# Moving the last five blocks of a routed expert layer into a conditional part

## The chip, the cores and the metric

The kernel runs on one core of a Trainium2 chip. The core has five engines that run their own instruction streams side by side: TensorE (PE in the profile, with its weight loads as PEld), VectorE (DVE), ScalarE (ACT), GpSimd (POOL) and SyncE (SP), which here issues most of the DMAs. The metric is the device time of one execution in microseconds. The kernel before took 1246.42 us, the median of three runs (1238.91, 1246.42 and 1249.45).

## The reference

The input x has 8 batches of 512 tokens with 512 features. Everything is fp32.

```python
xn = layernorm(x)
s  = gated_linear_attention(xn)     # 16 heads of 32, decay, chunks of 128, output projection
# the mixture, on the 4096 tokens of xn:
top4, e4 = top_k(softmax(xn @ gate_w.T), 4)          # 16 experts
w = top4 / top4.sum()
mixed  = sum over e of comb[:, e] * (silu(xn @ Wg[e]) * (xn @ Wu[e])) @ Wd[e]
shared = (silu(xn @ sWg) * (xn @ sWu)) @ sWd
ffn = mixed + shared * sigmoid(xn @ shared_gate_w)
out = x + s * silu(ffn)
```

Each token goes to 4 of 16 experts; an expert has two 512 to 128 matrices (gate and up) and one 128 to 512 matrix (down).

## The kernel before

The work stands in stages, written one after another in one function; a scheduling layer places the instructions of each engine and adds the semaphore waits.

The first stage normalizes all batches, writes the normalized rows to DRAM (`xn_d`), computes the router and the shared expert (kept in `sh_d`), and meanwhile runs attention for batch 0. `sort()` (L376 to 460) then works out where each of the 16384 (token, expert) pairs stands in lists that are sorted by expert. Each expert's list is padded to whole blocks of 128 rows, so the number of blocks that the lists fill depends on the data. The kernel provides for the most that can occur:

```python
NB = (B * N * TOPK + E * (P - 1)) // P      # L36: 143
```

In `sort()`, `nb` is the number of blocks of each expert and `end` (L412 to 414) their running sum, so that its last column is the number of blocks in use. From `end` it makes `eoff`, one expert number per block (held as the offset of that expert's weights, and as the column of its routing weight). `table()` makes `slot`, the token of each row of each block, while attention runs for batch 1.

The expert weights (`wexp`, 16 x 768 KB) are loaded in L969 to 970 and L979 to 980. Then comes the expert stage (L986 to 1100), one step for each of the 143 blocks, laid out as a software pipeline in the loop L1089 to 1098. For block i:

- `gather(i + 4)` (POOL): an indirect DMA fetches the rows of the block's 128 tokens. Seven buffers (`homes`) take turns.
- `turn_rows(i + 2)` (SP): a transposing DMA turns the 16-bit half of each row; `transpose_x(i + 2)` (TensorE) turns the fp32 half; `join(i + 1)` (ACT) puts both together as `xt`.
- `gate_up(i)`: TensorE loads the block's weight offset into a register (L1034) and multiplies (L1042, result `pgu`); ACT applies the Silu (L1046) and DVE the product (L1047), giving `slb`.
- `transpose_h(i - 1)`: TensorE turns `slb` (L1054), DVE copies it to `hT` (L1056).
- `down(i - 2)`: TensorE multiplies with the down matrix (L1063, `py`); DVE loads the column of the routing weight into a register (L1067) and scales the rows (L1072, `y`); SP stores them in `y_d` (L1074), 256 KB a block.

The `y` tiles come from the four buffers called `tmp`, which attention uses for its own scratch too.

The last stage (L1103 to 1207) runs attention for batches 2 to 7. It begins with `enter(2)`: keys (`pk`) and queries (`pq`) of batch 2 on TensorE (L598), with a Silu on ACT (L603) and a rotation on DVE (L605 to 609). Beside it `mixture` fetches the four expert rows of each token from `y_d` by indirect DMAs on POOL (L1121), adds them up, and `last` multiplies with the attention output and adds x. The transposed input of batch 3 (`xT_3`) is loaded by SP at the beginning of that stage (L538). All `y_d` gathers wait for the last stores to `y_d`. The order of each engine's instructions is that of the scheduling layer, except where a line says `behind(engine)` or `issue_after`, which pin an instruction behind an earlier one.

In the program as built, the first key matmuls of batch 2 stand before the last down projection of block 142 on TensorE, and the load of `xT_3` before the last store of `y` on SP.

Of the kernel before, what the change touches and what calls it, by code (L numbers as in the profile page):

```python
# [10 lines left out]
F32 = mybir.dt.float32  # L11
F16 = mybir.dt.float16
I32 = mybir.dt.int32
# [6 lines left out]
P = 128  # L20
B, N, D = 8, 512, 512
# [6 lines left out]
E, F, TOPK = 16, 128, 4  # L28
# [7 lines left out]
NB = (B * N * TOPK + E * (P - 1)) // P  # L36
WE = KC * 2 * F + D
TMP = 4
FIRST = 2
NBQ = -(-NB // 4)  # L40
QUAD = 4
GROUP = 16

# [51 lines left out]
def tile_block(ctx: ExitStack, tc: tile.TileContext, a: dict, out: bass.AP):  # L95
    nc = tc.nc
# [4 lines left out]
    const = ctx.enter_context(tc.tile_pool(name="const", bufs=1))  # L101
# [11 lines left out]
    y_d = dram.tile([NB * P, D], F32, name="y_d", tag="y_d")  # L113
# [23 lines left out]
    att = ctx.enter_context(tc.tile_pool(name="att", bufs=1, side="left"))  # L137
# [53 lines left out]
    sp = const.tile([P, 2, TOPK * NT], F16, tag="slot", name="sp")  # L191

    eoff = const.tile([P, 2, NBQ], I32, tag="eoff", name="eoff")

    def of_block(what, i):
        return eoff[i // NBQ * Q : i // NBQ * Q + 1, what, i % NBQ : i % NBQ + 1]
# [14 lines left out]
    def behind(engine):  # L211

        last = next(
            (i for i in reversed(nc.cur_bb.bb.instructions) if i.engine == engine), None)
        return tc.issue_after(last) if last else nullcontext()
# [160 lines left out]
    def sort():  # L376

        wt = p1.tile([P, NT, E], F32, tag="h1", name="wt", bufs=2)
        wr = p1.tile([P, NT, E], F32, tag="sl", name="wr", bufs=2)
        for r in range(TOPK):  # L380
            nc.gpsimd.tensor_tensor(
                wr if r else wt, oh[:, r].rearrange("p e t -> p t e"),
                w4[:, :, r : r + 1].to_broadcast([P, NT, E]), ALU.mult)
            if r:
                nc.gpsimd.tensor_tensor(wt, wt, wr, ALU.add)
        nc.sync.dma_start(
            xn_d[:, 2 * D :].rearrange("(t p) e -> p t e", p=P),
            wt.bitcast(U16))
        mf = mask.rearrange("p e t -> p (e t)")
        total = p1.tile([P, E * NT], F32, tag="lT", name="total", bufs=1)  # L390
        at = p1.tile([P, E, NT], F32, tag="at", name="at")
        af = at.rearrange("p e t -> p (e t)")
        for to, by, name in ((total, ones, "total"), (af, tri, "before")):
            ps = bank("a", f"p{name}")
            with on_pe():
                nc.tensor.matmul(ps, lhsT=by, rhs=mf, start=True, stop=True)
            nc.scalar.copy(to, ps)
        yield
        incl = p1.tile([P, E, NT], F32, tag="incl", name="incl")
        fl = incl.rearrange("p e t -> p (e t)")  # L400
        with behind(DVE):
            nc.vector.tensor_tensor_scan(fl, reset, total, 0.0, ALU.mult, ALU.add)

        ci = p1.tile([P, E], I32, tag="ci", name="ci")
        with behind(DVE):
            nc.vector.tensor_scalar(ci, incl[:, :, NT - 1], float(P - 1), None, ALU.add)
        with behind(DVE):
            nc.vector.tensor_scalar(ci, ci, 7, None, ALU.logical_shift_right)
        nb = p1.tile([P, E], F32, tag="nb", name="nb")
        with behind(DVE):  # L410
            nc.vector.tensor_copy(nb, ci)
        end = p1.tile([P, E], F32, tag="end", name="end")  # L412
        with behind(DVE):
            nc.vector.tensor_tensor_scan(end, ones[:, :E], nb, 0.0, ALU.mult, ALU.add)
        with behind(DVE):
            nc.vector.tensor_tensor(nb, end, nb, ALU.subtract)
        with behind(DVE):
            nc.vector.tensor_scalar(nb, nb, float(P), None, ALU.mult)
        yield

        with behind(DVE):
            nc.vector.tensor_tensor(fl, fl, total, ALU.subtract)
        with behind(DVE):
            nc.vector.tensor_tensor(af, af, fl, ALU.add)
        with behind(DVE):
            nc.vector.tensor_tensor(at, at, nb.unsqueeze(2).to_broadcast([P, E, NT]), ALU.add)
        yield
        oa = p1.tile([P, TOPK, E, NT], F32, tag="x", name="oa", bufs=3)
        pos = p1.tile([P, TOPK, NT], F32, tag="pos", name="pos")
        bl = p1.tile([P, 2, TOPK, NT], I32, tag="bl", name="bl")  # L430
        for r in range(TOPK):
            with behind(DVE):
                nc.vector.tensor_tensor(oa[:, r], oh[:, r], at, ALU.mult)
            with behind(DVE):
                nc.vector.tensor_reduce(
                    pos[:, r], oa[:, r].rearrange("p e t -> p t e"), axis=AX.X, op=ALU.add)
            with behind(DVE):
                nc.vector.tensor_copy(posi[:, r], pos[:, r])
            with behind(DVE):
                nc.vector.tensor_scalar(bl[:, 0, r], posi[:, r], P - 1, None, ALU.bitwise_and)  # L440
            with behind(DVE):
                nc.vector.tensor_scalar(bl[:, 1, r], posi[:, r], 7, None, ALU.logical_shift_right)
            with behind(DVE):
                nc.vector.tensor_copy(
                    sp.rearrange("p w (r t) -> p w r t", t=NT)[:, :, r], bl[:, :, r])
            yield

        cm = p1.tile([P, NBQ, E], F32, tag="xT1", name="cm", bufs=2)
        with behind(DVE):
            nc.vector.tensor_tensor(  # L450
                cm, end.unsqueeze(1).to_broadcast([P, NBQ, E]),
                iota_b.unsqueeze(2).to_broadcast([P, NBQ, E]), ALU.is_le)
        ef = p1.tile([P, NBQ], F32, tag="ef", name="ef")
        with behind(DVE):
            nc.vector.tensor_reduce(ef, cm, axis=AX.X, op=ALU.add)
        with behind(DVE):
            nc.vector.tensor_scalar(eoff[:, 0], ef, float(E - 1), float(WE), ALU.min, ALU.mult)
        with behind(DVE):
            nc.vector.tensor_scalar(eoff[:, 1], ef, float(E - 1), float(D), ALU.min, ALU.add)
        yield  # L460
# [507 lines left out]
    LATE = 4  # L968
    for e in range(E - LATE):  # L969
        nc.sync.dma_start(wexp[:, e, :], a["experts"][:, e, :])  # L970
    filling = table(wflat[:, (E - LATE) * WE :])
    next(filling)
    between[0] = lambda: next(filling, None)
# [5 lines left out]
    for e in range(E - LATE, E):  # L979
# [6 lines left out]
    blkp = left.enter_context(  # L986
        tc.tile_pool(name="blkp", bufs=1, side="left", reuse_waits="tile"))
    ROW = 2 * (D + E)
    more = att.tile([P, 2 * NC * D], U16, tag="v", name="more", bufs=2)
    homes = [blkp.tile([P, ROW], U16, tag=f"xg{j}", name=f"xg{j}") for j in range(4)]  # L990
    homes += [more[:, j * ROW : (j + 1) * ROW] for j in range(3)]
# [5 lines left out]
        return homes[i % len(homes)]  # L997

    def gather(i):
        if i < NB:  # L1000
            nc.gpsimd.indirect_dma_start(  # L1001
                out=row(i), out_offset=None, in_=xn_d,
                in_offset=bass.IndirectOffsetOnAxis(ap=slot[:, i : i + 1], axis=0))
# [2 lines left out]
        return pls[i % 2][:, i // 2 % 2]  # L1006

    def turn_rows(i):
        if i < NB:
            nc.sync.dma_start_transpose(turned(i), row(i)[:, D : 2 * D])  # L1010

    def transpose_x(i):
        if i < NB:
            pt_of[i] = bank("a", f"pt_{i}")
            for k in range(KP):
                nc.tensor.transpose(
                    pt_of[i][:, k * P : (k + 1) * P],
                    row(i).bitcast(F32)[:, k * P : (k + 1) * P], ident)

    def join(i):  # L1020
        if i < NB:
            xt = att.tile([P, KC, P], F32, tag="qT", name=f"xt_{i}", bufs=2)
            nc.scalar.copy(  # L1023
                xt[:, :KP, :].rearrange("p k t -> p (k t)"), pt_of.pop(i)[:, : KP * P])
            nc.scalar.copy(  # L1025
                xt[:, KP:, :].bitcast(U16).rearrange("p k (t h) -> p h k t", h=2),
                turned(i).rearrange("p (h k) t -> p h k t", h=2))
            xt_of[i] = xt

    def gate_up(i):  # L1030
        if not 0 <= i < NB:
            return
        with tc.issue_after(done[-1]) if done else nullcontext():
            _, (off_of[i],) = nc.values_load_multi_w_load_instructions(  # L1034
                of_block(0, i), engines=[mybir.EngineType.PE], min_val=0,
                max_val=(E - 1) * WE, bass_reorder=False,
# [11 lines left out]
        h_of[i] = sl  # L1048

    def transpose_h(i):  # L1050
        if not 0 <= i < NB:
            return
        ph = bank("a", f"ph_{i}")
        done.append(nc.tensor.transpose(ph[:, :P], h_of.pop(i), ident).ins)  # L1054
        hT = blkp.tile([F, P], F32, tag="hT", name=f"hT_{i}", bufs=2)
        nc.vector.tensor_copy(hT, ph[:, :P])  # L1056
        hT_of[i] = hT

    def down(i):
        if not 0 <= i < NB:  # L1060
            return
        py = bank("d", f"py_{i}")
        nc.tensor.matmul(  # L1063
# [22 lines left out]
            transpose_x(t - 2)  # L1086
    on_of.pop(FIRST - 1)
    join(0)
    for i in range(NB + 2):  # L1089
        turn_rows(i + 2)  # L1090
        join(i + 1)
        gate_up(i)
        if i == 2:
            gate_3(FIRST)
        transpose_x(i + 2)
        transpose_h(i - 1)
        down(i - 2)
        gather(i + 4)
    left.close()
    right.close()  # L1100

# [159 lines left out]
```

## Time and profile before

| | |
|---|---|
| median of three runs | 1246.42 us |
| profiled execution | 1229.7 us |
| its span, first to last instruction | 1227.9 us |
| mean granted TensorE clock | 0.991 |
| TensorE busy | 1177.3 us (96%) |
| VectorE busy | 768.2 us (63%) |
| GpSimd busy | 448.5 us (37%) |
| ScalarE busy | 407.3 us (33%) |
| expert matmuls L1042 | first 343.2 us, last 764.1 us |
| stores of y to `y_d`, issue to landing | 143, median 2.9 us |

In the profile a name such as `L1042 PE MATMUL pgu<-wexp,xt` is a group: line, engine, operation, written tile, read tiles. An entry of the order of time has the start, the length, the engine, the line and the count of merged records; a bracket says how long the engine stood idle before it and what released it. A fp32 matmul shows as two records, so that one block has eight `pgu` records and two `py` records. SPq, DVEq and the like are the instruction queue of an engine: register loads, semaphores and DMA issues, which are not counted as busy.

### The profile page before, as it was taken

To read this page: it belongs to the slowest core of one execution; us is meant where nothing else is said; L and a number is where in the kernel's file an instruction comes from. 1 tells how busy PE (TensorE), PEld (TensorE's weight loads), DVE (VectorE), ACT (ScalarE), POOL (GpSimd) and SP (SyncE) were. 2 spreads that over 40 slices of the span, in tenths; PEclk is the share of its full clock that TensorE was granted. 3 is DMA by queue.
4 is the path that set the end of the run, shared out by engine and by line. 5 is a ranking of instruction groups with operands and counts; after the bars stand their busy time and mean duration, and the time that the engine had idled before them with its cause. 6 is when DMAs were issued, how large, how long until landed. Compare 5 with 4: busy or idle time off the path is not lost. (4 is left out here: it accounts for less than half of the span.)

```text
span 1227.9 us, 21563 instructions
## 1 busy us (share of the span) xinstructions
PE 1177.3 (96%) x7799; PEld 696.7 (57%) x7799; DVE 768.2 (63%) x1652; ACT 407.3 (33%) x782; POOL 448.5 (37%) x430
## 2 busy tenths in 40 slices
PE   6998999989999999999999999999999999999997
PEld 3444554446467777777777776544554544445453
DVE  6378554899324444444444444887969789698784
ACT  3343333320264444444443443133141321411420
POOL 3222101100213333333333331581886857848211
PEclk9998999999999999999999999999999999999999
DMA  9784331181459999999999997950845636535012
GB/s 333 248 282 165 120 137 70 26 320 42 164 149 226 229 229 228 221 236 223 228 231 218 230 226 186 326 168 10 286 141 170 211 103 221 167 111 150 23 36 69
DMA packets 167719, 219.77 MB, mean 179 GB/s; under 512 B 93696, under 2 KB 102656, under 8 KB 165696
## 3 DMA queue, kind: packets, MB, share of 16 engines
q1 hardware_dynamic: 145936, 146.17, 40.3%
q0 software_dynamic: 21680, 72.23, 21.4%
q8 instruction: 64, 1.05, 0.3%
q14 instruction: 39, 0.32, 0.1%
HBM read 127.25 MB, written 72.35 MB: 163 GB/s over the span
## 5 line engine op out<-in xcount | busy, mean ns | idle before, releaser
L1042 PE MATMUL pgu<-wexp,xt 128*128 x1144 | 271.0, 380 | 2.4 <-ACT xt L1023 2.2
L1042 PEld LDWEIGHTS pgu<-wexp,xt 128*128 128x128 f32 x1144 | 216.5, 190 | 93.8 <-issue 31.4
L1001 POOL DMA_INDIRECT xg<-xn_d,slot x83 | 78.6, 947 | 281.0 <-DVE y L1072 168.1
L1047 DVE TENSOR_TENSOR slb<-slb,pgu 128x128 f32<-128x128 f32 x143 | 41.2, 288 | 205.8 <-ACT slb L1046 205.8
L1121 POOL DMA_INDIRECT yg<-y_d,posi x128 | 142.4, 1112 | 51.0 <-DMA m<-sh_d 23.5
L1025 ACT COPY xt<-pl 128x512 uint16<-128x512 uint16 x143 | 109.7, 767 | 148.5 <-DMA pl<-xg 92.1
L1063 PE MATMUL py<-wexp,hT 128*128 x286 | 146.4, 594 | 0.0
L556 PE MATMUL pv<-wv,xT 128*128 128x512 f32 x256 | 121.0, 611 | 4.3 <-DVE sh L370 2.6
L598 PE MATMUL pk<-xT,wk 128*128 128x512 f32 x256 | 121.9, 617 | 0.0
L598 PE MATMUL pq<-xT,wq 128*128 128x512 f32 x256 | 115.9, 593 | 0.0
L731 PE MATMUL pw<-wo,on 128*128 128x512 f32 x224 | 100.9, 596 | 1.8 <-ACT so L904 0.9
L1001 POOL DMA_INDIRECT more<-xn_d,slot x60 | 56.6, 943 | 115.9 <-DVE y L1072 111.2
L1153 POOL TENSOR_TENSOR xo<-xo,m 128x512 f32<-128x512 f32 x30 | 43.8, 1461 | 146.8 <-DVE m L1149 137.4
L1072 DVE TENSOR_SCALAR y<-py,xg 128x512 f32<-128x512 f32 x83 | 62.3, 750 | 30.4 <-PE py L1063 30.3
L556 PEld LDWEIGHTS pv<-wv,xT 128*128 128x128 f32 x256 | 46.4, 193 | 60.9 <-issue 55.2
L670 DVE TENSOR_TENSOR sc<-ps,dmask 128x512 f32<-128x512 f32 x128 | 79.4, 684 | 1.0 <-PE ps L654 1.0
L598 PEld LDWEIGHTS pq<-xT,wq 128*128 128x128 f32 x256 | 47.3, 191 | 52.2 <-issue 50.9
L598 PEld LDWEIGHTS pk<-xT,wk 128*128 128x128 f32 x256 | 46.9, 193 | 50.2 <-issue 47.7
L1046 ACT ACTIVATE slb<-pgu 128x128 f32<-128x128 f32 x143 | 39.8, 279 | 95.0 <-PE pgu L1042 94.9
L731 PEld LDWEIGHTS pw<-wo,on 128*128 128x128 f32 x224 | 41.2, 190 | 51.7 <-issue 44.7
L603 ACT ACTIVATE sk<-pk 128x512 f32<-128x512 f32 x32 | 19.1, 597 | 117.5 <-PE pk L598 102.1
L1072 DVE TENSOR_SCALAR y<-py,more 128x512 f32<-128x512 f32 x60 | 45.0, 750 | 19.8 <-PE py L1063 19.7
(166 smaller groups left out, 1751.1 us busy)
## 6 DMA issues: line engine op xcount, KB each, us to landing
y_d<-y SPq DMA_DIRECT2D x143, 256.0 KB, 2.9
wexp<-in_experts SPq DMA_DIRECT2D x16, 768.0 KB, 11.7
sh_d<-sh SPq DMA_DIRECT2D x32, 256.0 KB, 2.6
m<-sh_d SPq DMA_DIRECT2D x32, 256.0 KB, 4.5
xo<-in_x SPq DMA_DIRECT2D x32, 256.0 KB, 3.6
out<-xo SPq DMA_DIRECT2D x32, 256.0 KB, 2.1
x<-in_x SPq DMA_DIRECT2D x7, 1024.0 KB, 6.5
xT_d<-xT SPq DMA_DIRECT2D x7, 1024.0 KB, 5.1
```

The costliest lines, as they stand in the source:

```text
L556: nc.tensor.matmul(pv, lhsT=xT_of[b][:, k, t * P : (t + 1) * P], rhs=wv[:, k, :], start=(k == 0), stop=(k == KC - 1))
L598: nc.tensor.matmul(ps, lhsT=w[:, k, g * P : (g + 1) * P], rhs=xT_of[b][:, k, :], start=(k == 0), stop=(k == KC - 1))
L670: nc.vector.tensor_tensor(s, pss[j].rearrange("p (c t) -> p c t", t=C), dmask[:, g * HG + j].unsqueeze(1).to_broadcast([P, NC, C]), ALU.mult)
L731: nc.tensor.matmul(pw, lhsT=on_of[b][:, g, t * P : (t + 1) * P], rhs=wo[:, g, :], start=(g == 0), stop=(g == G - 1))
L1001: nc.gpsimd.indirect_dma_start(out=row(i), out_offset=None, in_=xn_d, in_offset=bass.IndirectOffsetOnAxis(ap=slot[:, i : i + 1], axis=0))
L1025: nc.scalar.copy(xt[:, KP:, :].bitcast(U16).rearrange("p k (t h) -> p h k t", h=2), turned(i).rearrange("p (h k) t -> p h k t", h=2))
L1042: nc.tensor.matmul(pg[:, : 2 * F], lhsT=xt[:, k, :], rhs=wflat[:, bass.ds(off + k * 2 * F, 2 * F)], start=(k == 0), stop=(k == KC - 1))
L1047: nc.vector.tensor_tensor(sl, sl, pg[:, F : 2 * F], ALU.mult)
L1063: nc.tensor.matmul(py, lhsT=hT_of.pop(i), rhs=wflat[:, bass.ds(off_of.pop(i) + KC * 2 * F, D)], start=True, stop=True)
L1072: gone.append(nc.vector.tensor_scalar(y, py, row(i).bitcast(F32)[:, bass.ds(at, 1)], None, ALU.mult).ins)
L1121: nc.gpsimd.indirect_dma_start(out=yg, out_offset=None, in_=y_d, in_offset=bass.IndirectOffsetOnAxis(ap=posi[:, r, g : g + 1], axis=0))
L1153: nc.gpsimd.tensor_tensor(xo, xo, m, ALU.add)
```

## The change

Blocks 0 to 137 are written out as before. Blocks 138 to 142 move into a part of the program that is entered only if the lists fill more than 138 blocks. For that, `sort()` keeps the number of blocks in use as an integer (`filled`), and after the first 138 blocks every engine loads it into a register and branches. Inside the part the pipeline is filled anew for the five blocks. Since the rows of those blocks in `y_d` would otherwise never be written when the part is skipped, they are filled with zeros earlier, after the first twelve expert loads, from a `tmp` tile that GpSimd clears.

In the program as built, every engine has the register load and the branch behind its work for block 137. On the path that skips the part each engine waits for its own last work, and SP for all of its DMAs, and then raises its semaphores to the values that the part would have left. The instructions of the last stage stand behind that on each engine; otherwise their order is that of before. The five stores of zeros stand on SP between the twelfth expert load and the load of `xT_2`.

```diff
+SURE = NB - 5
...
+    filled = const.tile([P, 1], I32, tag="filled", name="filled")
...
             nc.vector.tensor_tensor_scan(end, ones[:, :E], nb, 0.0, ALU.mult, ALU.add)
+        with behind(DVE):
+            nc.vector.tensor_copy(filled, end[:, E - 1 : E])
...
     for e in range(E - LATE):
         nc.sync.dma_start(wexp[:, e, :], a["experts"][:, e, :])
+    none = att.tile([P, D], F32, tag="tmp", name="none", bufs=TMP)
+    nc.gpsimd.memset(none, 0.0)
+    for i in range(SURE, NB):
+        nc.sync.dma_start(y_d[i * P : (i + 1) * P, :], none)
...
+    span = [0, SURE]
...
     def gather(i):
-        if i < NB:
+        if i < span[1]:
...
     def gate_up(i):
-        if not 0 <= i < NB:
+        if not span[0] <= i < span[1]:
             return
...
-    for i in range(NB + 2):
-        turn_rows(i + 2)
-        join(i + 1)
-        gate_up(i)
-        if i == 2:
-            gate_3(FIRST)
-        transpose_x(i + 2)
-        transpose_h(i - 1)
-        down(i - 2)
-        gather(i + 4)
+    def blocks(others=lambda i: None):
+        for i in range(span[0], span[1] + 2):
+            turn_rows(i + 2)
+            join(i + 1)
+            gate_up(i)
+            others(i)
+            transpose_x(i + 2)
+            transpose_h(i - 1)
+            down(i - 2)
+            gather(i + 4)
+
+    blocks(lambda i: gate_3(FIRST) if i == 2 else None)
+    _, (count,) = nc.values_load_multi_w_load_instructions(
+        filled[:1, :1], min_val=0, max_val=NB,
+        skip_runtime_bounds_check_because="the lists fill at most NB blocks")
+    with tc.If(count > SURE):
+        span[:] = SURE, NB
+        done.clear()
+        gone.clear()
+        for i in range(SURE, SURE + 4):
+            gather(i)
+        for i in range(SURE, SURE + 2):
+            turn_rows(i)
+            transpose_x(i)
+        join(SURE)
+        blocks()
```

The tests of the other helpers (`turn_rows`, `transpose_x`, `join`, `transpose_h`, `down`) change in the same way as those shown.

## The prediction

> **What bounds the kernel now.** I read the page's busy slices first, then a table of stretches, then the order of time around the end of the expert stage, then what TensorE waited for after it.
>
> From the page, the busy shares and the TensorE slices:
>
> ```profile
> PE 1177.3 (96%) x7799; PEld 696.7 (57%) x7799; DVE 768.2 (63%) x1652; ACT 407.3 (33%) x782; POOL 448.5 (37%) x430
> PE   6998999989999999999999999999999999999997
> L1042 PE MATMUL pgu<-wexp,xt 128*128 x1144 | 271.0, 380 | 2.4 <-ACT xt L1023 2.2
> ```
>
> TensorE is busy nearly everywhere, and the expert matmuls (L1042, eight records a block, 1144 / 8 = 143 blocks) waited 2.4 us in the whole stage. The stretches say the same of a middle piece of the stage and of its end (columns: busy us per engine with records, granted clock, DMA share, GB/s):
>
> ```profile
> 400.00:500.00 100.00, 99.99 (x445) 74.22 (x444) 41.73 (x104) 42.77 (x103) 32.07 (x34) 1.00 0.95 229
> 762.56:770.52 7.96, 7.96 (x26) 4.29 (x24) 3.69 (x7) 0.28 (x1) 0.00 (x0) 1.00 0.45 128
> ```
>
> The second row runs from the first matmul of block 142 to the first of the queries (pq) of batch 2: 7.96 us without a hole. The chain that ended last holds one DVE addition only, so I use the order of time instead:
>
> ```profile
> 691.24 1.89 PE L1042 MATMUL pgu<-wexp,xt 128*128 x8
> ...
> 743.71 1.89 PE L1042 MATMUL pgu<-wexp,xt 128*128 x8
> ...
> 749.54 1.89 PE L1042 MATMUL pgu<-wexp,xt 128*128 x8
> 752.67 1.99 PE L1042 MATMUL pgu<-wexp,xt 128*128 x8
> 756.84 1.99 PE L1042 MATMUL pgu<-wexp,xt 128*128 x8 [1.00 <-ACT xt L1023]
> 759.86 1.89 PE L1042 MATMUL pgu<-wexp,xt 128*128 x8
> 762.56 1.89 PE L1042 MATMUL pgu<-wexp,xt 128*128 x8
> ...
> 766.13 0.28 DVE L1056 COPY hT<-ph 128x128 f32<-128x128 f32 x1
> 766.23 1.02 PE L598 MATMUL pk<-xT,wk 128*128 128x512 f32 x2
> 767.09 1.02 PE L1063 MATMUL py<-wexp,hT 128*128 x2
> 767.94 2.74 PE L598 MATMUL pk<-xT,wk 128*128 128x512 f32 x6
> 768.15 0.75 DVE L1072 TENSOR_SCALAR y<-py,xg 128x512 f32<-128x512 f32 x1 [0.97 <-PE py L1063]
> ```
>
> From 691.24 to 749.54 lie 20 blocks: 58.30 / 20 = 2.915 us each. Late blocks 139 and 140 came 3.13 and 4.17 us after their forerunners, a hiccup of 1.5 us from late row transposes. Where the last block's down projection must wait for the DVE copy, TensorE runs the first two key matmuls of the next stage (pk at 766.23). After 765 us all idle time of TensorE matmuls sums to under 10 us, so time saved here should reach the end.
>
> **What the Trainium skill says.** "Advanced Engine Details and Errata", Control Flow Timing: a branch about 51 ns, a compare-and-branch about 108 ns; the trace of before shows neither. "DMA: Bandwidth & Descriptors", Latency and other measured facts: a register load has a floor near 600 ns; this trace differs (second row below, median 305 ns), and I use the trace. "Runtime: NRT & Kernel Launch", Instruction fetch mechanics: instructions stream in pages of 16 KB, 256 instructions, and a taken branch to a page that is not held waits for a DMA; the instruction queue of the trace fits the size (1.05 MB in 64 packets, 16.4 KB each), the stall no run here shows. "SBUF — State Buffer", Who interferes with whom: GpSimd and VectorE share one exclusive port pair, though a GpSimd instruction that only writes does not hold up the second operand of a VectorE one.
>
> ```profile
> L1072 DVEq EVENT_SEMAPHORE  x144: 21/50/50, 353.0 to 766.9; - x144
> L1067 DVEq TENSOR_LOAD <-eoff x143: 299/305/1021, 250.3 to 766.4; - x143
> ```
>
> **The change, part by part.** Is the part entered? Counting each token's four largest router logits on the reference's inputs, the experts get 929 to 1082 tokens; the counts rounded up to blocks of 128 sum to 136. 136 is not above 138: it is skipped.
>
> *Five blocks fewer.* 5 x 2.915 = 14.58 us of TensorE time off the path. Their gathers, row transposes and stores go too. Blocks 136 and 137 become the run-out, in the shape that 141 and 142 had.
>
> *The run-out loses its cover.* Let T0 be the first matmul of the last block. Before, T0 = 762.56; the last hT copy ends at 766.41 (T0+3.85), the last py then stands behind a key pair until T0+4.53, and pq starts at T0+7.96. In the changed program nothing from after the part may stand inside: order on TensorE is py_136, py_137, load of the count, branch, then pk. So py_137 starts about T0+4.0 and its record ends T0+5.05; its y multiply on DVE (0.75) ends T0+5.85. The skipping path adds waits: each engine waits for its own last work and then raises its semaphores to what the part would have left. The first pk waits for DVE's raised count, so for the last y. Behind DVE's wait no compute of DVE's is due, since its next work (swk) needs pk anyway. With 0.05 for each semaphore step (row above) pk starts at T0+6.1; eight passes at 0.43 (3.44 for the eight, from 767.94 + 6 x 0.43 = 770.52) bring pq to T0+9.55. Loss 9.55 - 7.96 = 1.6 us.
>
> *Load and branches.* DVE's load (0.305) and compare-and-branch (0.11) run on its sequencer while the 0.75 us multiply executes; TensorE's run beside it as well. Cost 0 with that cover, 0.4 us without. Bounds for fetching: below, nothing (a gain is excluded, nothing is removed); above, one landing of a store (2.9 us in the page's DMA list stands in for a page) for each of two taken branches on TensorE: pk at T0+10.4, so 4.3 more. The jump passes about 165 TensorE instructions (26 matmul and load records a block, plus registers), fewer than the 256 of a page, so I take zero, page presumably held.
>
> *SP and GpSimd at the part.* SP waits until the last y store has landed (issue about T0+6.0, plus 2.9), then releases GpSimd's gathers and the load of xT_3. Queued behind SP's wait: xT_3 and the m loads. xT_3 goes from T0+5.6 to about T0+9.3, 3.7 later, but its first reader (pv at 803.90) is 35 us off. The first yg gather was at 775.17 = T0+12.6 because the last store stood behind the 1 MB xT_3; now about T0+9.3, so GpSimd gets earlier, not later. ACT's first Silu needs HW semaphores SP raises about T0+8; pk's result comes at T0+9.6. Cost 0; if landings took 5 us more, ACT would be late by some 3.
>
> *Zero writes.* Five stores of 256 KB join SP's queue behind the first twelve expert loads (last issue about 263.5), ahead of xT_2 at 286.67. 1.31 MB at the 422 GB/s that the stretch 260 to 270 shows take 3.1 us in a queue idle for 23 us: cost 0, bounded by 3.1 if all of it delayed xT_2, for which TensorE already waits 1.66 us at 292.18. The GpSimd memset of the zeros (no row; a 128x512 addition there takes 1.46) runs beside DVE's mask work, which TensorE then waits for: 0 to 1.3, I take 0.1. The one-column copy on DVE: 0.18 as the neighbouring 128x16 subtraction, 0.1 of it exposed. Holding a tmp buffer delays nothing I find: its next user waits for the five stores about 35 us after they land.
>
> *Sum.* -14.6 + 1.6 + 0 + 0.2 = -12.8; I write -12.4, leaving 0.4 for the uncovered branch. The profiled execution takes 1229.7 us (span 1227.9, 1.8 around it), 1.3% below the median of the three runs, 1246.42, with no view telling why. Against itself it would fall to about 1217.3, or 1215.8 if its hiccup does not recur. Against the median: 1234.0.
>
> **Rivals.**
> *Page refetch* (25%): one or both taken branches wait for instructions. For: the jumps are the program's first inside it. Against: short jump. Gain 12.4 - 2.4 to 12.4 - 4.3: 1236 to 1239.
> *More than the sum* (14%): hiccups of 1.5 us and a slower steady pace in the timed runs go with the blocks, and earlier gathers help the last stage. For: blocks 139 and 140. Against: TensorE hardly waits later. Gain 14 to 16: 1230 to 1232.
> *Slower* (7%): after the branch each engine restarts its instruction stream cold. Place: between py_137 and pk. Price: serial fetches of 2.9 us on DVE, then TensorE, and again as they run on with no page ahead. From five such fetches in a row (14.5 us) it cancels the gain; eight give 1257. The part entered after all would end there too, through the same drain and a refill of gather (4.2), transpose (3.6) and joins: 1258. Against: 136 leaves two blocks of room.
>
> **How the numbers follow.** The forecast has 54%. A measurement of this kernel can tell about 1%, 12.5 us, from no change, and the forecast sits on that edge: half of its cases pass it, all of the second rival's do, the first's do not. Faster 0.45, same 0.48, slower 0.07. The three runs spread by 10.5 us, so I widen 1230 to 1239 by some 4 either way: 1226 to 1243.
>
> **What would show it.** Right: 138 blocks at 2.915; a hole in TensorE of about 0.3 us before py_137 and 1.2 us before pk; pk about 6.1 us after T0; first yg gather 9 to 10 us after T0. A hole of 3 us or more with no work beside it means fetching. Any pgu beyond 1104 records means the part was entered. A longer idle at 292 would blame the zero stores. Wrong altogether if idle time appears later, in TensorE's waits after the part, instead of the end moving in.

## The result and the profile after

Over six timed runs of each kernel, the kernel before took 1247.57 us (median, 1238.91 to 1251.24) and the changed one 1230.04 us (1228.61 to 1231.55): ratio 0.9869, 95% interval 0.9836 to 0.9902. That is 17.5 us less where 12.4 were forecast; the interval, 12.2 to 20.5 us, just takes the forecast in. The profiled execution of the changed kernel took 1229.93 us (span 1228.1), near its median, while that of the kernel before had taken 1229.7. So the two traces end at the same time although the timed runs differ by 17.5 us. Much of what follows is about that contradiction.

The page of the changed kernel, the busy shares, the TensorE slices and the group of the gate and up products:

```profile
PE 1170.0 (95%) x7734; PEld 690.8 (56%) x7734; DVE 754.3 (61%) x1638; ACT 401.5 (33%) x767; POOL 441.8 (36%) x426
...
PE   6998999989989999999999999999999999999997
...
L1051 PE MATMUL pgu<-wexp,xt 128*128 x1104 | 261.4, 380 | 0.8 <-ACT xt L1032 0.8
```

1104 / 8 = 138 blocks: the conditional part was skipped. The same line had 1144 records before. The next view has the two stretches that the prediction showed, a middle piece of the expert stage and the run-out from the first gate product of the last block (T0) to the first query product (pq) of batch 2:

```profile
400.00:500.00 100.00, 99.80 (x444) 74.28 (x443) 42.28 (x104) 42.92 (x102) 32.11 (x34) 1.00 0.94 229
746.29:756.50 10.21, 8.46 (x25) 4.12 (x24) 3.69 (x7) 0.28 (x1) 0.23 (x1) 1.00 0.29 105
```

The middle is as full as before. The run-out takes 10.21 us instead of 7.96, and TensorE is busy for 8.46 of them: a hole has come in. The order of time shows where:

```profile
746.29 1.89 PE L1051 MATMUL pgu<-wexp,xt 128*128 x8
...
749.09 2.22 PE L1072 MATMUL py<-wexp,hT 128*128 x4
...
751.36 0.75 DVE L1081 TENSOR_SCALAR y<-py,more 128x512 f32<-128x512 f32 x1 [0.45 <-PE py L1072]
...
752.99 3.67 PE L602 MATMUL pk<-xT,wk 128*128 128x512 f32 x8 [1.68 <-DVEq L1113]
...
756.27 0.95 POOL L1146 DMA_INDIRECT yg<-y_d,posi  x1 [19.25 <-SPq L1113]
756.50 1.02 PE L602 MATMUL pq<-xT,wq 128*128 128x512 f32 x2
```

The key products (pk) no longer stand between the last two down projections (py), and they start 6.70 us after T0 instead of 3.67. They were released by VectorE's queue at L1113, the line of the branch. The first gather of expert rows (yg) stands 9.98 us after T0, where the kernel before had it at 12.6. What VectorE's queue did in that time is in the view of the line of the load of the count (queue, operation, min/median/max in ns, first and last start in us), and in that of the branch:

```profile
L1110 POOLq TENSOR_LOAD <-filled x1: 497/497/497, 735.8 to 735.8; - x1
L1110 ACTq TENSOR_LOAD <-filled x1: 573/573/573, 748.2 to 748.2; - x1
L1110 PEldq TENSOR_LOAD <-filled x1: 486/486/486, 750.2 to 750.2; - x1
L1110 DVEq TENSOR_LOAD <-filled x1: 801/801/801, 751.4 to 751.4; - x1
L1110 SPq TENSOR_LOAD <-filled x1: 539/539/539, 752.5 to 752.5; - x1
```

```profile
L1113 PEldq COMPARE_BRANCH  x1: 368/368/368, 750.8 to 750.8; - x1
L1113 DVEq COMPARE_BRANCH  x1: 72/72/72, 752.6 to 752.6; - x1
```

VectorE's load starts with the last y product at 751.4 and takes 0.80 us, more than the 0.75 us that were to cover it. The branch follows at 752.6, the semaphore steps after it, and TensorE goes on at 752.99. Of the two holes that the prediction named, the one before the last py is 0.07 us (10.21 - 8.46 - 1.68; 0.3 forecast) and the one before pk 1.68 us (1.2 forecast). No engine shows a stall of microseconds that could be a fetch of instructions.

### The profile page after: what moved, and what is told of

The parts are those of the page before. It is cut to its first block, busy times and chain, and to the rows that moved or that the text cites. A ratio compares the mean times of both kernels' runs of the same rounds, so it can differ in the third digit from the quotient of the medians.

```text
span 1228.1 us, 21368 instructions
## 1 busy us (share of the span) xinstructions
PE 1170.0 (95%) x7734; PEld 690.8 (56%) x7734; DVE 754.3 (61%) x1638; ACT 401.5 (33%) x767; POOL 441.8 (36%) x426
## 5 line engine op out<-in xcount | busy, mean ns | idle before, releaser
L1051 PE MATMUL pgu<-wexp,xt 128*128 x1104 | 261.4, 380 | 0.8 <-ACT xt L1032 0.8
L1051 PEld LDWEIGHTS pgu<-wexp,xt 128*128 128x128 f32 x1104 | 209.0, 190 | 88.5 <-issue 42.8
L1010 POOL DMA_INDIRECT xg<-xn_d,slot x80 | 75.9, 949 | 248.5 <-DVE y L1081 162.5
L1034 ACT COPY xt<-pl 128x512 uint16<-128x512 uint16 x138 | 105.8, 766 | 140.2 <-DMA pl<-xg 86.8
L1072 PE MATMUL py<-wexp,hT 128*128 x276 | 141.3, 594 | 0.1
L560 PE MATMUL pv<-wv,xT 128*128 128x512 f32 x256 | 123.5, 622 | 5.2 <-DVE sh L372 4.1
L564 ACT COPY v<-pv 128x512 f32<-128x512 f32 x32 | 18.8, 588 | 122.2 <-PE pv L560 118.3
```

The source lines that it names most:

```text
L560: nc.tensor.matmul(pv, lhsT=xT_of[b][:, k, t * P : (t + 1) * P], rhs=wv[:, k, :], start=(k == 0), stop=(k == KC - 1))
L1010: nc.gpsimd.indirect_dma_start(out=row(i), out_offset=None, in_=xn_d, in_offset=bass.IndirectOffsetOnAxis(ap=slot[:, i : i + 1], axis=0))
L1034: nc.scalar.copy(xt[:, KP:, :].bitcast(U16).rearrange("p k (t h) -> p h k t", h=2), turned(i).rearrange("p (h k) t -> p h k t", h=2))
L1051: nc.tensor.matmul(pg[:, : 2 * F], lhsT=xt[:, k, :], rhs=wflat[:, bass.ds(off + k * 2 * F, 2 * F)], start=(k == 0), stop=(k == KC - 1))
L1072: nc.tensor.matmul(py, lhsT=hT_of.pop(i), rhs=wflat[:, bass.ds(off_of.pop(i) + KC * 2 * F, D)], start=True, stop=True)
```

## The experiments

Two theories stood after the result. *Sum*: the change is worth the time of five blocks less what the run-out grew, about 12.3 us, and the rest of the 17.5 is scatter. *More than the sum*: the kernel before loses time somewhere else too, and the change removes that. Three groups of four kernels were run, each group on one chip and beside the kernel before: on chips 11, 1 and 13, by the numbers of the record, where the kernel before takes 1229, 1247 and 1229 us. For the first comparison and for the profile of before no chip is noted. Each group ran at another time too, so whether such a level belongs to the chip is not shown; the text speaks of the lower and the higher level. In the tables, pk and pq are counted from T0, and "last stage" runs from that first pq to the end of the span, in the profiled execution.

**First group, where the kernel before takes 1229.28 us** (1225.44 to 1234.77, 19 runs).

| kernel | median us | ratio to before, 95% | pk | pq | last stage |
|---|---|---|---|---|---|
| before | 1228.69 | 0.9997, 0.998 to 1.0014 | 3.67 | 7.96 | 457.4 |
| changed | 1217.18 | 0.9898, 0.9873 to 0.9922 | 6.70 | 10.21 | 459.7 |
| changed, no branch | 1211.71 | 0.9863, 0.9832 to 0.9893 | 3.67 | 7.96 | 456.7 |
| changed, 136 blocks | 1210.23 | 0.9843, 0.9816 to 0.9869 | 6.70 | 11.90 | 461.2 |

*The kernel before against itself*, no edit.

> The kernel before, unchanged, against itself. Sum theory (the change is worth 14.6 us of blocks less the 2.25 us that the run-out grew, 12.3 us; the other 5 us of the 17.5 measured are scatter of the kernel before): ratio 1.000 with an interval of about 0.005 to each side, single times between 1229 and 1251 us, and the place of the scatter is the last stage (its length differs by up to 15 us between profiled executions, 457.4 us in the one shown, while the first 742 us differ by under 3). More-than-the-sum theory (the kernel before has a real loss that the change removes beside the blocks): its runs stay near 1246 us, the profiled execution shown (1229.7) was the outlier, and a new profile shows the loss.

The ratio is 1. But single times lie between 1225.06 and 1234.77, not up to 1251. Neither theory had that: the level of the kernel before had moved by 18 us. By its time (1229.7 us) and its last stage (457.4 us) the profile of before that the prediction used belongs to this level, not to that of the timed runs beside it.

*The changed kernel again*, no edit.

> The changed kernel, unchanged, once more. Sum theory: 12 to 13 us below the kernel before on the same chip (ratio 0.990), pq of the last stage 10.2 us after the first gate and up product of block 137's successor place, as in its first profile. More-than-the-sum theory: again 17 us below (ratio 0.986) and again a narrow spread of about 3 us against some 10 for the kernel before.

12.1 us below, and the run-out the same to 0.01 us: the sum's figure. The pair of traces accounts for it. T0 moved from 765.18 to 749.48 us (-15.70), the run-out grew by 2.25, the last stage by 2.3; together -11.2, the difference of the spans (1230.5 and 1219.3).

*Without load, test and conditional part*: the last five blocks are left out for good.

```diff
-    _, (count,) = nc.values_load_multi_w_load_instructions(
-        filled[:1, :1], min_val=0, max_val=NB,
...
-    with tc.If(count > SURE):
...
```

> The changed kernel without the load of the count, the test and the conditional part: 138 blocks always, the last five blocks are left out for good; the zero writes and the copy of the count stay. Theory that the load and the branch outlast the cover of the last y product: the first pk of the last stage comes 0.5 to 1.7 us sooner after the last block's first gate product than the 6.70 us of the changed kernel, the first pq as much (9.0 to 9.6 us instead of 10.21), and the time is 0.6 to 2 us below the changed kernel. Rival (the run-out without its cover costs this much by itself, the branch nothing): pk stays at 6.5 to 6.7 us and the time within 0.3 us.

The direction was right and the size was not: pq came 2.25 us sooner instead of 0.6 to 1.2, because with no branch the two key products go back between the last down projections. And the time fell by 5.5 us, not 2. So the branch costs more than its own hole. The two traces lie further apart than the medians, by 9.3 us, but 4.1 of that came ahead of T0, where the programs are alike (the changed kernel's trace has two more stretches of half clock there, each 3.4 us long, at 340 and 354 us). Behind T0 there is, beside the run-out, the last stage: 456.7 against 459.7 us. Its TensorE instructions are the same, in the same order, and the lag between the two traces grows at two places only before the 803 us mark of the changed kernel's trace: the transposes of the rotated keys (pk from kT) come 1.10 us late at 787 us and another 0.65 late at 800 us. The same waits recur in the third group, which is where I show them. Right behind them the clock record of this trace has half the clock for 3.4 us, at 801 us, which costs 1.7. With the 2.25 of the run-out and the 1.75 of the two waits that makes 5.7 us, near the 5.5 of the medians.

*136 blocks ahead of the test*, seven in the part.

```diff
-SURE = NB - 5
+SURE = NB - 7
```

> The changed kernel with 136 blocks ahead of the test instead of 138 (seven in the conditional part, still not entered, since 136 are filled). Sum theory: two blocks of 2.915 us less, 5.8 us below the changed kernel, and the run-out and the branch the same (pk at 6.7 us, pq at 10.2 us). More-than-the-sum theory, where what was gained beside the blocks came with the end of the stage moving away from a slow stretch of the last stage: the step is not 5.8 us but anything from 0 to 10, and the last stage's length changes with its start.

7.0 us below the changed kernel, 5.8 expected from two blocks. pk at 6.70 us is right; pq at 11.90 is off by 1.7, since a stretch of half clock (3.4 us from 747.6 us) fell on the eight key products, which took 5.37 us instead of 3.67.

**Second group, where the kernel before takes 1247.02 us** (1240.94 to 1257.27, 43 runs).

| kernel | median us | ratio to before, 95% | pk | pq | last stage |
|---|---|---|---|---|---|
| changed, gathers delayed | 1230.92 | 0.9861, 0.9834 to 0.9888 | 6.70 | 10.21 | 472.7 |
| changed, count loaded early | 1229.64 | 0.9866, 0.9836 to 0.9896 | 6.02 | 9.53 | 473.8 |
| 143 blocks, branch | 1246.15 | 0.9995, 0.9978 to 1.0013 | 3.67 | 7.96 | 472.1 |
| 143 blocks, zero writes | 1245.75 | 0.9984, 0.9963 to 1.0004 | 3.67 | 7.96 | 467.3 |

*Gathers delayed*, the question being whether the earlier gathers make the two waits.

```diff
             yg = comb.tile([P, D], F32, tag="yg", name=f"yg_{b}_{t}_{r}", bufs=14)
+            if (b, t, r) == (FIRST, 0, 1):
+                for _ in range(8):
+                    nc.gpsimd.memset(yg, 0.0)
```

> The changed kernel with eight memsets of 128x512 (0.52 us each by the one that the changed kernel has, 4.2 us in all) on GpSimd between the first and the second gather of expert rows in the last stage. Port theory (after the branch the gathers and with them GpSimd's sums of expert rows come about 4 us earlier against TensorE's work than in the kernel before; a sum that runs beside a two-input VectorE operation holds that one up for 2.1 us instead of 0.68, now on the way to TensorE): the sums stand again as in the kernel before, the two waits of TensorE for kT in the first batch of the last stage (1.0 and 0.65 us) are gone, and the time is 1.5 to 3.5 us below the changed kernel. Rival (the waits come from the branch itself or from the load of x that now comes 2 us later): they stay, and the time is that of the changed kernel or up to 1 us above it.

The gathers did move, the second from 1.0 us after pq, in the changed kernel's first trace, to 6.1, but the time is that of the changed kernel at this level (1230.04 us in the first comparison). It doesn't decide the matter. At this level the changed kernel has neither of the two waits in its first profile: other gaps (below) come before them, which would give VectorE the time. There was nothing here for the delay to remove. At the other level it wasn't tried.

*Count loaded early*, at block 100, on all five engines.

```diff
+        if i == 100:
+            with behind(DVE), behind(ACT), behind(POOL), \
+                    behind(mybir.EngineType.SP), behind(mybir.EngineType.PE):
+                counts.append(nc.values_load_multi_w_load_instructions(
+                    filled[:1, :1], min_val=0, max_val=NB, bass_reorder=False,
...
-    _, (count,) = nc.values_load_multi_w_load_instructions(
...
```

> The changed kernel with the count loaded into the registers of all five engines in the middle of the blocks (at block 100) instead of after the last one; the branch stays. Theory that the load of the count on VectorE (0.80 us in the trace) outlasts the last y product and so holds TensorE's first pk: pk at 6.1 us after the last block's first gate product instead of 6.70, pq at 9.6 instead of 10.2, and the time 0.6 us below the changed kernel. Rival (the branch itself is what holds it, or the time lies in the order of the instructions): pk stays at 6.6 to 6.7 us, the time within 0.3 us.

The run-out of this kernel in the order of time, and VectorE's branch:

```profile
744.52 1.89 PE L1051 MATMUL pgu<-wexp,xt 128*128 x8
...
749.58 0.75 DVE L1081 TENSOR_SCALAR y<-py,more 128x512 f32<-128x512 f32 x1 [0.45 <-PE py L1072]
...
750.54 3.67 PE L602 MATMUL pk<-xT,wk 128*128 128x512 f32 x8 [0.99 <-DVEq L1123]
...
754.05 3.17 PE L602 MATMUL pq<-xT,wq 128*128 128x512 f32 x7
```

```profile
L1123 DVEq COMPARE_BRANCH  x1: 72/72/72, 749.6 to 749.6; - x1
```

The branch now runs at 749.6, at the start of the last y product and beside it. pk is at 6.02 us and pq at 9.53, both 0.68 sooner, so the load was what outlasted its cover. The whole time can't show 0.7 us here.

*143 blocks and a branch*: the conditional part holds one memset and is not entered.

```diff
-    span = [0, SURE]
+    span = [0, NB]
...
     with tc.If(count > SURE):
-        span[:] = SURE, NB
...
-        blocks()
+        spare = blkp.tile([P, P], F32, tag="sl", name="spare", bufs=2)
+        nc.vector.memset(spare, 0.0)
```

> All 143 blocks as in the kernel before, then the load of the count, the test and a conditional part with one small memset, not entered; the zero writes stay (they are overwritten). Branch theory: pq of the last stage 10.2 us after the last block's first gate product instead of 7.96 (2.25 us), and the first batch of the last stage 1.6 to 3.3 us longer by earlier gathers: 4 to 5.5 us slower than the kernel before (ratio 1.003 to 1.0045). Sum theory of the prediction (the branch hides): within 1 us of the kernel before.

No cost of the branch can be seen (the interval is -2.7 to 1.6 us, where 4 to 5.5 were expected), and pq is at 7.96 us. The first gather of expert rows stands 4.5 us behind pq, as in the kernel before, so the second cost has no occasion here either. The reason is the place of the branch: this part uses nothing of the blocks, so the scheduler put the branch into the last blocks' work, with products queued behind it. The views of its two lines:

```profile
L1110 PEldq TENSOR_LOAD <-filled x1: 487/487/487, 765.0 to 765.0; - x1
L1110 DVEq TENSOR_LOAD <-filled x1: 537/537/537, 765.6 to 765.6; - x1
```

```profile
L1113 PEldq COMPARE_BRANCH  x1: 230/230/230, 765.6 to 765.6; - x1
L1113 DVEq COMPARE_BRANCH  x1: 72/72/72, 766.2 to 766.2; - x1
```

VectorE and TensorE load and branch here while TensorE's products follow one another without a hole: busy for all 7.96 us from T0 at 765.03. So it isn't the branch that costs 2.25 us in the changed kernel; it is that nothing from behind it can fill the run-out ahead of it, and that VectorE's load stands last.

*143 blocks with the zero writes*, the memset and the copied count, no branch.

> All 143 blocks, with the five zero writes, the memset and the copy of the count, without load, test and conditional part. Prediction's step (they hide): ratio 1.000, at most 0.3 us. Upper bound of that step: 3.1 us slower (ratio 1.0025).

Ratio 0.9984, at most 1.0004: the bound of 3.1 us (1.0025) is excluded, and the forecast of 0.2 us lies within the interval (-4.6 to 0.5 us). TensorE's wait for xT at 292 us was 1.0 us in this trace, 1.7 in that of before.

**Third group, where the kernel before takes 1228.68 us** (1225.27 to 1233.78, 19 runs).

| kernel | median us | ratio to before, 95% | pk | pq | last stage |
|---|---|---|---|---|---|
| before | 1229.90 | 1.001, 0.9995 to 1.0025 | 3.67 | 7.96 | 457.2 |
| changed | 1219.77 | 0.9925, 0.9902 to 0.9947 | 6.69 | 10.20 | 460.5 |
| changed, no branch | 1214.66 | 0.9876, 0.9848 to 0.9904 | 3.67 | 7.96 | 456.3 |
| 136 blocks, early count | 1213.65 | 0.9858, 0.983 to 0.9886 | 6.02 | 9.53 | 460.6 |

The kernel before, the changed one, the one without a branch, and 136 blocks with the early count (the two edits above together):

> The kernel before once more with a profile. The chips or placements behind the two calls so far differ: where the kernel before takes 1229 us its profiles show a last stage of 457.4 us, where it takes 1247 us the profiles of the other kernels show last stages of 467 to 474 us, with gaps of 0.3 to 0.7 us before TensorE's small matmuls in which it waits for nothing that the profile shows. Theory that this is a property of where the program runs, whatever the kernel: at 1247 us this profile too has the gaps and a last stage of 467 to 474 us; at 1229 us it has none, and 457 us. Rival (the gaps come with the zero writes, the branch or the gathers): 457 us in both places.

> The changed kernel once more beside it. Where the kernel before takes 1229 us: 12 us below it, last stage 459 to 461 us by waits of 1 to 1.7 us for VectorE's rows that run into GpSimd's sums. Where it takes 1247 us: 16 to 17 us below it, last stage 470 to 474 us; the profiles then tell how much of the difference lies ahead of the last stage (13 to 15 us by the counts so far) and how much in it.

> 138 blocks with no load of the count, test or conditional part (the last five blocks are left out), once more beside the changed kernel. Branch theory: 2.25 us sooner at the first pq of the last stage in either place, and the last stage shorter by the 1.6 us of waits for VectorE's rows where these can be seen: 3 to 6 us below the changed kernel. Rival (the 5.5 us of the first comparison was chance of the throttle): 2 us or less.

> 136 blocks ahead of the test, seven in the conditional part, and the count loaded in the middle of the blocks. Sum theory: 5.8 us for the two blocks and 0.7 us for the load, 6.5 us below the changed kernel, and 18 to 24 us below the kernel before, by the place. Rival (two blocks nearer to the end of the filled ones bring a new wait): less than 4 us below the changed kernel.

The level was again the lower one, so the kernel before gave no profile at 1247 us. At 1229 us its last stage takes 457.2 us without gaps, as expected. The changed kernel is 8.9 us below it, 12 expected (interval 6.5 to 12.0). Without the branch it is 5.1 us better, inside the expected 3 to 6, so the 5.5 of the first group recurs; of the two differences (5.2 and 5.0 us in the means) 1.7 and 1.9 us go with the granted clock, by the estimate below, and 3.5 and 3.1 us do not. 136 blocks with the early count are 6.1 us below the changed kernel, 6.5 expected.

What TensorE waited for in the first batch of the last stage, from its first pq to the next batch's, by the table of waits (us in total, times, longest). The kernel before:

```profile
PE pk L625 <- DVE state L659: 1.6, 1, 1.6
```

The changed kernel:

```profile
PE pk L629 <- DVE state L663: 3.3, 2, 2.3
```

The changed kernel without a branch:

```profile
PE pk L629 <- DVE state L663: 1.3, 1, 1.3
```

One wait of 1.3 to 1.6 us without the branch, two of together 3.3 us with it: 1.7 us more than in the kernel before, in this group as in the first. The new one is the first, 1.03 us; the other is 0.65 us longer than before. What releases them is VectorE's state update (L663), which reads the tile pk that the transposes are to overwrite. It stands behind VectorE's row of operations on keys and queries. Ahead of the place of the new wait the row reads in the kernel before (order of time, from 20 us after pq):

```profile
791.21 0.69 DVE L609 TENSOR_TENSOR kT<-kT,swk 128x512 f32<-128x512 f32 x1
...
794.25 2.15 DVE L609 TENSOR_TENSOR qT<-qT,swq 128x512 f32<-128x512 f32 x1
794.57 1.28 POOL L1127 TENSOR_TENSOR yg<-yg,yg 128x512 f32<-128x512 f32 x1
```

and in the changed kernel:

```profile
774.42 2.06 DVE L613 TENSOR_TENSOR kT<-kT,swk 128x512 f32<-128x512 f32 x1
774.63 1.29 POOL L1152 TENSOR_TENSOR yg<-yg,yg 128x512 f32<-128x512 f32 x1
...
778.59 1.28 POOL L1155 TENSOR_TENSOR yg<-yg,yg 128x512 f32<-128x512 f32 x1
778.87 1.56 DVE L613 TENSOR_TENSOR qT<-qT,swq 128x512 f32<-128x512 f32 x1
...
780.92 0.52 DVE L663 SCALAR_TENSOR_TENSOR state<-state,lamc,pk 128x32 f32<-128x32 f32 x2
...
781.50 0.33 PE L629 MATMUL pk<-ident,kT 128*128 128x128 f32 x1 [1.03 <-DVE state L663]
```

The same two-input operation takes 0.69 us alone and 2.06 us when a GpSimd sum of expert rows runs inside it. The Trainium skill, "SBUF — State Buffer", Who interferes with whom, has the two engines share one exclusive port pair, and the numbers agree with that: 0.69 + 1.29 = 1.98. (It is VectorE's operation that is held up, though by the trace it started 0.21 us before the sum.) In the kernel before one operation of this row was hit; with the branch GpSimd's work starts earlier against TensorE's (the first gather 0.10 instead of 4.62 us after pq, the first sum 9.46 instead of 12.44), and two are hit ahead of a transpose that TensorE is waiting for. That the earlier gathers are the cause is read from the traces, and without the branch both the early gathers (first at 4.5 us after pq again) and the new wait are gone. But that run takes the branch away with them, and the one that was to delay the gathers alone fell where the waits don't show, so it is not shown by an experiment of its own.

**What stays open.** At the higher level all five profiles I have (the changed kernel's first and the second group's four) have last stages of 467 to 474 us, and TensorE's waits over that stage show gaps ahead of small products. The changed kernel:

```profile
PE pk L647 <- issue: 5.0, 12, 0.5
PE ps L658 <- issue: 3.4, 11, 0.5
```

143 blocks with a branch:

```profile
PE po L692 <- issue: 2.6, 4, 1.0
PE ps L658 <- issue: 2.1, 6, 0.9
PE pk L647 <- issue: 1.9, 5, 0.5
```

"issue" means that TensorE waited for nothing that the profile shows. None of the nine profiles at the lower level has such gaps in the last stage, whatever the kernel. They go with the level of the run and not with the change, since the 143-block kernels have them too; what they are, the records don't say. A profile of the kernel before at this level is missing.

Why the gain is larger at this level the traces don't tell: between the two 143-block kernels of the second group (spans 1245.1 and 1236.7) and the changed kernel's first profile (1228.1) they give 17.0 and 8.6 us, while the medians give 16.1 and 15.7. The timed runs tell more, since each has its mean granted clock on record. Span times (1 - clock) is an estimate of what stretches of half clock took from a run. Averaged over the runs it is:

| | before, mean us | clock's share | changed, mean us | clock's share | gain | gain without the clock's share |
|---|---|---|---|---|---|---|
| first group | 1229.2 | 10.8 | 1217.6 | 12.4 | 11.6 | 13.2 |
| third group | 1229.0 | 10.2 | 1219.1 | 13.6 | 9.9 | 13.3 |
| second group, gathers delayed | 1247.0 | 15.9 | 1230.4 | 14.1 | 16.6 | 14.8 |
| second group, count loaded early | 1247.0 | 15.9 | 1230.8 | 14.1 | 16.2 | 14.4 |

So the granted clock accounts for most of the difference between the levels: at the lower one it takes more from the changed kernel, at the higher one more from the kernel before. With five or six runs of each changed kernel the last column is good to about 1 us (standard error). The clock doesn't explain the higher level itself: without its share the kernel before still takes 12.3 to 12.7 us more there. Why the clock falls this way is open.

## Why the prediction was right, and where it was not

*Five blocks, 14.58 us: right, with the hiccup on top.* In the third group's trace of before the last five blocks take 14.36 us from block 137's first product (748.77) to block 142's (763.13). The last of them is the shorter run-out step of 2.70 us, which the changed kernel has too in another place, so 14.36 + 0.22 = 14.58. In four other traces with 143 blocks it is 15.20 to 15.94: the late row transpose that holds up one of blocks 138 to 140 comes often, adds 0.8 to 1.6 us, and goes with the blocks. The rival "more than the sum" was right on that. Over all traces T0 stands at 763.5 us in the mean with 143 blocks (five traces) and at 746.5 with 138 (seven), 17.0 us apart; single traces scatter by 4 to 6 us there, so the term is 14.6 to 17, with the forecast at its lower end.

*The run-out, 1.6 us: mechanism right, 2.25 measured.* What failed is the step "Cost 0 with that cover, 0.4 us without" for load and branch. The load was priced at the 305 ns of the block loads; VectorE's took 801 ns and outlasted the 0.75 us product. The figure of the Trainium skill that the prediction set aside, a floor near 600 ns in "DMA: Bandwidth & Descriptors", Latency and other measured facts, was nearer, though it is no floor: the count's loads took 464 to 939 ns. With the load out of the way pk stands at 6.02 us and pq at 9.53, where the prediction had 6.1 and 9.55. The 0.4 that was set aside for an uncovered branch met most of the missing 0.65.

*Page refetch, 25%, and cold streams, 7%: no sign of either.* TensorE's compare-and-branch took 0.37 us, the others' 0.05 to 0.07, and there is no hole but the one explained. The Trainium skill, "Advanced Engine Details and Errata", Control Flow Timing, has about 0.11 us for it, between the two.

*SP and GpSimd, cost 0: wrong.* The first gather came at 9.98 us as forecast (9 to 10), "so GpSimd gets earlier, not later"; from that followed no cost, and in the rival even a gain. At the lower level the earlier sums run into VectorE's row and TensorE loses some 1.75 us; the loss is measured, that the gathers cause it is argued. The load of xT_3, later as forecast, did no harm that the traces show.

*Zero writes, memset, copied count, 0.2: not contradicted* by the run that has nothing else (-4.6 to 0.5 us).

*The sum.* With the measured terms it is 14.58 - 2.25 - 1.75 = 10.6 us, 11.4 to 12.2 with a hiccup. The two comparisons at the lower level gave 12.1 and 8.9. There the forecast's 12.4 was 0.3 us off in one and 3.5 in the other. That it came so near in the one is in part luck: two costs that it missed were met by the hiccup and the 0.4 set aside. With the 17.0 us of the mean T0 in place of 14.58 the sum is 13.0, near the 13.2 and 13.3 us that are left without the clock's share.

*The base.* The step "Against the median: 1234.0" subtracted a gain that was worked out on a trace of one level (1229.7) from runs at another (1246.42). The prediction noted it "with no view telling why"; the runs now say that the two belong to different levels. At the level of the timed runs the gain is 16 to 17.5 us, so the 1230.04 us is what the rival "more than the sum" named (1230 to 1232), not the forecast's 1234.0. It lies inside 1226 to 1243, but for a reason that neither named: what the gain has more here goes for the most part with the granted clock. That much is luck. The two traces of before and after, of different levels, even show the prediction's sign for "wrong altogether": T0 came 16.3 us sooner and the last stage grew from 457.4 to 471.6 us. Only pairs of one level show the end moving in. Against the level of its own trace the prediction had named 1217.3; the changed kernel takes 1217.18 and 1219.77 there.

*A better version.* With 136 blocks ahead of the test the kernel takes 1210.23 us beside 1217.18 of the changed one, and with the early count 1213.65 beside 1219.77: 0.984 and 0.986 of the kernel before. For the given inputs 136 is exactly what is filled, by the prediction's count; one more block would enter the part, whose price was not measured.

## What to carry to other kernels

A part that is skipped isn't priced by what it skips alone: no work from behind the branch stood ahead of it here, so what had filled the run-out was lost (1.57 of the 2.25 us), while a branch with independent work on both sides showed no cost. What every engine needs for the test should be loaded long before it, and an engine off the critical path that starts sooner must be followed to the ports it shares. Before a gain is subtracted from a median, see that the profile and the median are of the same level, and before two gains are compared, what share the granted clock has in each.

## What was not expected of the hardware

- The same program took 1229 us in two groups (chips 11 and 13) and 1247 in another (chip 1), with gaps of up to 1.0 us ahead of TensorE's small products in the latter.
- The load of the one count took 464 to 576 ns on ScalarE and GpSimd, 485 to 826 on TensorE, 532 to 939 on SyncE and 537 to 817 on VectorE, where the blocks' own loads on VectorE have a median of 305.
- TensorE's compare-and-branch took 230 to 373 ns where the others' took 50 to 72.
- TensorE's clock was granted at half for stretches of mostly 3.4 or 6.8 us; one of 3.4 us that fell on the key products made them 1.7 us longer. In three of the four traces with the unentered part at the lower level such a stretch came at 792 to 801 us, at or right behind the second wait for the tile pk, and in three of four at the higher level, where those waits hardly show (0 to 0.2 us), at 783 to 799 us. None of the six traces without the part has one there. So it comes without that wait too; what brings it is open.
